# Three edits to the order and the split of ScalarE's work in a graph-attention kernel

## The chip, the cores and the metric

The kernel runs on one core of one Trainium2 chip. The metric is the device time of one execution in microseconds; lower is better. Times are medians of several runs of the same program.

## What is computed

Three attention layers over a graph of 6250 nodes (256 numbers each) and 100,000 edges (`src`, `dst`, sorted by `dst`). The first two are one GATv2 block with four heads of 64, the third is a GAT layer with eight heads of 32. After the second and the third layer the input is added and the row is normalised. Each node also has an edge from itself in the first two layers.

```python
def _gatv2_layer(x, src, dst, n, Wl, Wr, att, b):
    xl = (x @ Wl).reshape(n, H, C)
    xr = (x @ Wr).reshape(n, H, C)
    e = leaky_relu(xl[src] + xr[dst], 0.2)
    logits = einsum('ehc,hc->eh', e, att)
    ex = exp(logits - segment_max(logits, dst)[dst])
    alpha = ex / segment_sum(ex, dst)[dst]
    return segment_sum(xl[src] * alpha[:, :, None], dst).reshape(n, H * C) + b

h = elu(_gatv2_layer(x, ...))          # layer one
x = layernorm(x + _gatv2_layer(h, ...))  # layer two
x = layernorm(x + gat_layer(x, ...))     # layer three
```

## The kernel before, in words

A plan (the first 220 us) sorts the nodes by degree and cuts them into 49 blocks of 128, one node to a partition. A block has as many columns as its largest node has edges: 38 in the first block, 25, 24, 23 in the next ones, 9 in the last, 814 in all. A column is one neighbour of each of the 128 nodes.

`layer2` runs the first two layers (i = 0 and i = 1), each as one loop over the 49 blocks. The order of the instructions on every engine is the order in which the program writes them: nothing is rescheduled. In iteration b of the loop stand, in this order:

- `start(b + 3)`: layer one gathers the block's neighbour lists and inputs into `near` (x1 is the part of it with the inputs) by a GpSimd DMA; layer two loads the block's rows of two tables by SP.
- `gather(b + 1)`: one GpSimd DMA for each column of the next block, 128 rows of a table into a row tile `g` (L1207). A row tile holds up to T = 9 columns, and there are nine of them. A block of S columns (its neighbours and the node itself) is cut into chunks of equal size, at most nine columns each.
- `ready(b + 1)`: the next block's own rows. In layer one (`own1`) TensorE transposes x1 (L1254), ScalarE copies the result to `xT` (L1256), TensorE makes the products `pl` and `pr` (L1261). In layer two (`own2`) ScalarE copies both from the loaded tile. `pr` goes to PSUM; the copy of the own row into the first column of `g` is put off to `later`.
- `attend(b)`: for each chunk VectorE makes z = max(g, pr), z times the attention vector, and its sum over each head (L1396 to L1398); then the maximum over the columns (L1272). ScalarE takes the exponential of each of the four heads with the sum into `den` (L1279), copies the weights of the last `few` columns to SBUF (`by`, L1286), does what is in `later` (L1477 or L1517), and in layer one casts a column of places (L1408).
- `end(b - 1)`: VectorE scales the sum of the block before by its `den` into `h` (L1415). In layer one (`finish1`) ScalarE makes the two parts of the ELU (L1481 to L1484); in layer two (`finish2`) VectorE takes mean and variance and ScalarE makes the deviation by Ln and Exp (L1350, L1351).
- VectorE takes the reciprocal of `den` (L1447).
- `weighted_sum`: for each chunk VectorE multiplies the rows by the weights (L1309), and TensorE adds the columns up in PSUM by products with the identity (`acc`, L1316). The last `few` columns of the last chunk are multiplied by ScalarE, a head at a time (L1308). After the first chunk's product `between` calls the rest of the block before: in layer one VectorE adds the parts of the ELU (L1489), in layer two it scales the mean (L1355) and ScalarE normalises (L1358).
- `last`, of the block before: TensorE transposes h, ScalarE copies it to `xT`, TensorE makes the products with the next layer's weights, ScalarE copies these to a row (L1496, or L1531 and L1532 in layer two), and SP writes the row to the next layer's tables in HBM.

Two blocks before the end of a layer, `follow` issues the first gathers of the next layer, which read the rows of all but the last blocks (`begin`). Layer three has a loop of its own, with VectorE's sums in place of TensorE's, and isn't touched.

Of the kernel before, what the change touches and what calls it, by code (L numbers as in the profile page):

```python
# [26 lines left out]
F32 = mybir.dt.float32  # L27
# [8 lines left out]
P = 128  # L36
# [1092 lines left out]
def tile_by_degree(  # L1129
# [3 lines left out]
    nc = tc.nc  # L1133
# [3 lines left out]
    NB = -(-N // P)  # L1137
# [3 lines left out]
    W2 = H2 * (D2 + 1)  # L1141
# [16 lines left out]
    x1 = near[:, :, CM:]  # L1158
# [43 lines left out]
    def gather_rows(b, rows, cut, own, table, of, width, j0, j1):  # L1202


        for g, (s0, s1) in zip(rows, cut):
            for j in range(max(s0 - own, j0), min(s1 - own, j1)):
                nc.gpsimd.indirect_dma_start(  # L1207
                    out=g[:, j + own - s0, :width], out_offset=None, in_=table,
                    in_offset=source(of, b, j),
                )  # L1210

    def row_tiles(b, own):
        cut = chunks(cols[b] + own)
        return [rowp.tile([P, T, RW], F32, name="g") for _ in cut], cut
# [33 lines left out]
            nc.vector.reduce_sum(bad, pb, axis=AX.X)  # L1248
            nc.vector.tensor_single_scalar(done, bad, 0.0, op=OP.is_equal)

    def transposed(work, ps, xt):
        pt = ps.tile([P, 2, P], F32, name="pt", tag="tp")
        for c in range(2):
            nc.tensor.transpose(pt[:, c, :], xt[:, c * P : (c + 1) * P], ident)  # L1254
        xT = work.tile([P, 2, P], F32, name="xT")
        nc.scalar.copy(xT, pt)  # L1256
        return xT

    def product(pm, xT, w):
        for c in range(2):  # L1260
            nc.tensor.matmul(pm, xT[:, c, :], w[:, c, :], start=c == 0, stop=c == 1)  # L1261
# [6 lines left out]
    def weights(work, ps, lg, S, H, scalar=0):  # L1268


        top = work.tile([P, H], F32, name="top")
        nc.vector.tensor_reduce(  # L1272
            top, lg[:, :S, :].rearrange("p s h -> p h s"), axis=AX.X, op=OP.max, negate=True
        )
        wt = ps.tile([P, S, H], F32, name="wt")
        den = work.tile([P, H], F32, name="den")
        if H <= 4:
            for h in range(H):
                nc.scalar.activation(  # L1279
                    wt[:, :, h], lg[:, :S, h], AF.Exp, bias=top[:, h : h + 1],  # L1280
                    accum_out=den[:, h : h + 1],
                )
            by = None
            if scalar:
                by = work.tile([P, scalar, H], F32, name="by")
                nc.scalar.copy(by, wt[:, S - scalar :, :])  # L1286
            return (wt, by), lambda: den
        nc.vector.tensor_add(lg[:, :S, :], lg[:, :S, :], top[:, None, :].to_broadcast([P, S, H]))
        nc.scalar.activation(wt, lg[:, :S, :], AF.Exp)  # L1289

        def add_up():
            nc.vector.reduce_sum(den, wt.rearrange("p s h -> p h s"), axis=AX.X)
            return den

        return (wt, None), add_up
# [64 lines left out]
    def layer2(i, table, of, width, start, own, finish, follow):  # L1360

        with ExitStack() as es:
            zp = es.enter_context(tc.tile_pool(name=f"z{i}", bufs=1))
            work = es.enter_context(tc.tile_pool(name=f"work{i}", bufs=3))
            ps = es.enter_context(tc.tile_pool(name=f"ps{i}", bufs=2, space=PSUM))
            ps1 = es.enter_context(tc.tile_pool(name=f"ps1{i}", bufs=1, space=PSUM))  # L1370
            pst = es.enter_context(tc.tile_pool(name=f"pst{i}", bufs=2, space=PSUM))
            at = ps1.tile([P, W2], F32, name="at")
            nc.scalar.copy(at, att[i])
            state = {}

            def gather(b):
                first = EARLY[b] if b in begun else 0
                rows, cut = begun.pop(b) if first else row_tiles(b, 1)
                gather_rows(b, rows, cut, 1, table, of, width, first, cols[b])
                state[b] = [rows, cut]  # L1380

            later = []

            def ready(b):
                pr, put = own(work, ps, pst, b, state[b][0][0][:, 0, :W2])
                state[b].append(pr)
                later.append(put)

            def attend(b):
                rows, cut, xr = state.pop(b)  # L1390
                S = cols[b] + 1
                lg = work.tile([P, CM + 1, H2], F32, name="lg")
                for g, (s0, s1) in zip(rows, cut):
                    n = s1 - s0
                    z = zp.tile([P, T, W2], F32, name="z")[:, :n, :]
                    nc.vector.tensor_max(z, g[:, :n, :W2], xr[:, None, :].to_broadcast([P, n, W2]))  # L1396
                    nc.vector.tensor_mul(z, z, at[:, None, :].to_broadcast([P, n, W2]))  # L1397
                    nc.vector.reduce_sum(  # L1398
                        lg[:, s0:s1, :], z.rearrange("p t (h d) -> p t h d", h=H2), axis=AX.X
                    )  # L1400
                few = min(S // 3, cut[-1][1] - cut[-1][0] - 1) if b + 1 < NB else 0
                wt, new = weights(work, ps, lg, S, H2, few)
                while later:
                    later.pop()()
                if i == 0:
                    for g, (s0, s1) in zip(rows, cut):
                        s = max(s0, 1)
                        nc.scalar.copy(spots[:, b, s - 1 : s1 - 1], g[:, s - s0 : s1 - s0, W2])  # L1408
                    if 0 < b <= len(EARLY):
                        sort_sources(work, pst, b - 1)  # L1410
                return rows, cut, wt, new

            def end(b, acc, den):
                h = work.tile([P, F], F32, name="h")
                nc.vector.tensor_mul(  # L1415
                    per_head(h, H2), per_head(acc, H2),
                    den.unsqueeze(2).to_broadcast([P, H2, D2]),
                )
                if i == 0:
                    nc.vector.tensor_add(h, h, bias[0])  # L1420
                return finish(work, pst, b, h)

            for b in range(3):
                if (i, b) not in loaded:
                    start(b)
            gather(0)
            ready(0)
            later.pop()()
            if i == 0:
                none(state[0][2])  # L1430
            acc, den, rest = None, None, None
            for b in range(NB):
                if b + 3 < NB:
                    start(b + 3)
                if b + 1 < NB:
                    gather(b + 1)
                if b + 2 == NB:
                    follow()
                if b + 1 < NB:
                    ready(b + 1)  # L1440
                rows, cut, wt, new = attend(b)
                if b:
                    rest = end(b - 1, acc, den)
                if i == 0:
                    nc.vector.tensor_add(x1[:, b, :], x1[:, b, :], bias[1])
                den = new()
                nc.vector.reciprocal(den, den)  # L1447

                last = []

                def between():
                    if b:
                        last.append(rest())

                acc = weighted_sum(ps1, rows, cut, wt, H2, D2 + 1, between)
                if i == 0 and b + 1 < NB:
                    none(state[b + 1][2])
                if last:
                    last[0]()
            end(NB - 1, acc, den)()()  # L1460

    def none(t):
# [5 lines left out]
            out=near[:, b, :], out_offset=None, in_=near_d[:, :], in_offset=node(b)  # L1468
        )

    def own1(work, ps, pst, b, row):
        xT = transposed(work, pst, x1[:, b, :])
        pl = pst.tile([P, W2], F32, name="pl", tag="tp")
        product(pl, xT, wc[0][:, 0])
        pr = ps.tile([P, W2], F32, name="pr")
        product(pr, xT, wc[0][:, 1])
        return pr, lambda: nc.scalar.copy(row, pl)  # L1477

    def finish1(work, pst, b, h):
        neg = work.tile([P, F], F32, name="neg")  # L1480
# [29 lines left out]
        nc.sync.dma_start(two[:, 1, :], xr2_d[b * P : (b + 1) * P])  # L1510
        kept[b] = two

    def own2(work, ps, pst, b, row):
        two = kept.pop(b)
        pr = ps.tile([P, W2], F32, name="pr")
        nc.scalar.copy(pr, two[:, 1, :])
        return pr, lambda: nc.scalar.copy(row, two[:, 0, :])  # L1517

    def finish2(work, pst, b, h):
        nc.vector.tensor_add(h, h, x1[:, b, :])  # L1520
# [18 lines left out]
    kept, loaded = {}, set()  # L1539
# [11 lines left out]
    with ExitStack() as es:  # L1551
        work = es.enter_context(tc.tile_pool(name="work3", bufs=3))
        ps = es.enter_context(tc.tile_pool(name="ps3", bufs=3, space=PSUM))
        state = {}
# [50 lines left out]
        acc, den, puts, rest = None, None, {}, None  # L1605
        for b in range(NB):
# [4 lines left out]
            rows, cut, wt, new = attend(b)  # L1611
            if b:
                rest = end(b - 1, acc, den)
# [39 lines left out]
```

## Time and profile before

| | |
|---|---|
| median of 3 runs | 3907.3 us (3907.01 to 3914.32) |
| profiled execution | 3906.24 us, span 3904.4 us |
| layer one | 220.6 to 1476.1 us |
| layer two | 1476.1 to 2710.9 us |
| layer three | 2710.9 to 3904.4 us |
| busy over the span | VectorE 2859.7, GpSimd 2558.8, TensorE 1465.1, ScalarE 1093.2 us |
| mean granted TensorE clock | 0.669 |

The bounds of the layers are the ends of VectorE's reciprocals (L1447), of which there is one to a block: the first and the last of layer one, and the last of layer two. In a group of instructions the columns are line, engine, operation, tiles and shapes, count; then busy time and mean ns of one; then the idle time of the engine just before them, with what ended most of it. In a timeline they are start, duration, engine, line, operation, tiles, shapes and count, and in brackets the idle time before it. DVE is VectorE, ACT ScalarE, PE TensorE's matmuls, PEld its weight loads, POOL GpSimd. A releaser called "issue" or "remote" is one that the profile can't name.

### The profile page before, as it was taken

The page shows a single profiled execution, that of the slowest core. Times are in us where ns is not written, and L with a number is a line of the kernel's source. Part 1 is how long each engine was busy: PE and PEld are TensorE (multiplying, and loading weights), DVE is VectorE, ACT ScalarE, POOL GpSimd, SP SyncE. Part 2 cuts the span into 40 slices and gives each one's busy share as a digit, 9 for nine tenths or more (in the row PEclk, how much of TensorE's full clock was granted, in tenths as well). Part 3 has the DMA queues.
Part 4 walks back from the last instruction along what each step waited for, and adds up shares of the span by engine and source line. Part 5 has one row for each costly group of instructions (what it writes and reads, how often), then busy time and mean ns, then how long its engine had stood idle before and what let it go on. Part 6 is the DMA issues. An engine that isn't in the chain of part 4 may idle for free.

```text
span 3904.4 us, 23669 instructions
## 1 busy us (share of the span) xinstructions
PE 1465.1 (38%) x5147; PEld 1100.0 (28%) x5147; DVE 2859.7 (73%) x2624; ACT 1093.2 (28%) x4179; POOL 2558.8 (66%) x2642
## 2 busy tenths in 40 slices
PE   5335655646667653355545455554000000000000
PEld 4223443435455542243433334442000000000000
DVE  6267888768888867798877889895686666666655
ACT  2123433434445441243334334442000000000000
POOL 6466666666666654666666666663777777777774
PEclk8667787777888886676766777776555555555555
DMA  8443333333334333333434344342433333333332
GB/s 192 101 94 100 104 103 100 105 102 103 105 103 107 104 102 71 103 106 105 112 104 111 107 110 111 109 111 69 100 107 105 97 96 97 97 97 96 97 97 56
DMA packets 197563, 399.62 MB, mean 102 GB/s; under 512 B 63516, under 2 KB 115994, under 8 KB 197396
## 3 DMA queue, kind: packets, MB, share of 16 engines
q0 software_dynamic: 123488, 342.06, 33.7%
q1 hardware_dynamic: 66226, 54.22, 4.9%
q10 hardware_dynamic: 7698, 1.74, 0.4%
q8 instruction: 45, 0.74, 0.1%
q14 instruction: 106, 0.87, 0.1%
HBM read 357.84 MB, written 40.42 MB: 102 GB/s over the span
## 4 chain that ended last, share of the span: by engine, by line
issue 24%; POOL 21%; PE 16%; DVE 14%; another core or an unknown queue 12%; ACT 9%; DMA 2%; DVEq 0%; SPq 0%; ACTq 0%; POOLq 0%
POOL g L1207 19%; PE acc L1316 10%; ACT g L1308 4%; PE pm L1261 3%; DVE z L1397 3%; DVE z L1396 3%; DVE lg L1398 3%; ACT wt L1279 2%; DVE weighted L1327 1%; DVE g L1309 1%; DMA g<-xl_d,near_r 1%; POOL out L1597 1%; ACT xT L1256 1%; PE pl L1261 1%
## 5 line engine op out<-in xcount | busy, mean ns | idle before, releaser
L1207 POOL DMA_INDIRECT g<-xl_d,near_r x1591 | 1508.6, 948 | 843.6 <-issue 455.7
L1316 PE MATMUL acc<-g,ident 128*128 128x256 f32 x3452 | 1015.0, 455 | 910.1 <-issue 361.4
L1316 PEld LDWEIGHTS acc<-g,ident 128*128 128x128 f32 x3452 | 768.0, 229 | 1152.9 <-issue 617.4
L1207 POOL DMA_INDIRECT g<-whs_d,near_r x777 | 802.2, 1032 | 293.9 <-issue 251.9
L1308 ACT ACTIVATE g<-g,by 128x64 f32<-128x64 f32 x2064 | 550.4, 337 | 331.3 <-issue 328.0
L1396 DVE TENSOR_TENSOR z<-g,pr 128x1820 f32<-128x1820 f32 (+4 forms) x236 | 503.4, 2133 | 39.3 <-DMA g<-xl_d,near_r 25.7
L1397 DVE TENSOR_TENSOR z<-z,at 128x1820 f32<-128x1820 f32 (+4 forms) x236 | 503.7, 2134 | 8.1
L1398 DVE TENSOR_REDUCE lg<-z 128x28 f32<-128x1820 f32 (+4 forms) x236 | 503.6, 2134 | 8.1
L1336 DVE TENSOR_REDUCE acc_v<-weighted 128x256 f32<-128x4096 f32 (+16 forms) x49 | 349.2, 7127 | 11.7 <-remote 6.1
L1309 DVE TENSOR_TENSOR g<-g,wt 128x1792 f32<-128x1792 f32 (+5 forms) x236 | 353.8, 1516 | 2.9
L1567 DVE TENSOR_TENSOR lg<-g,s_r 128x56 f32<-128x56 f32 (+4 forms) x113 | 22.8, 214 | 367.4 <-DMA g<-whs_d,near_r 300.0
L1289 ACT ACTIVATE wt<-lg 128x128 f32<-128x128 f32 (+17 forms) x49 | 14.0, 285 | 901.2 <-DVE top L1272 309.9
L1256 ACT COPY xT<-pt 128x256 f32<-128x256 f32 x147 | 55.0, 374 | 704.8 <-remote 367.3
L1327 DVE TENSOR_TENSOR weighted<-g,wt 128x1792 f32<-128x1792 f32 (+4 forms) x113 | 229.5, 2048 | 0.0
L1447 DVE RECIPROCAL den<-den 128x4 f32<-128x4 f32 x98 | 17.4, 177 | 226.8 <-ACT wt L1279 158.9
L1279 ACT ACTIVATE wt<-lg,top 128x19 f32<-128x19 f32 (+14 forms) x392 | 116.1, 296 | 209.0 <-DVE top L1272 83.7
L1415 DVE TENSOR_TENSOR h<-acc,den 128x256 f32<-128x256 f32 x98 | 40.7, 416 | 166.8 <-remote 122.3
L1261 PE MATMUL pm<-wh_cat,xT 128*128 128x272 f32 x196 | 83.9, 568 | 192.7 <-issue 108.7
L1261 PE MATMUL pm<-wcat,xT 128*128 128x260 f32 x392 | 138.5, 512 | 45.8 <-ACT xT L1256 44.8
L1261 PEld LDWEIGHTS pm<-wcat,xT 128*128 128x128 f32 x392 | 96.9, 261 | 82.1 <-ACT xT L1256 61.7
L1261 PEld LDWEIGHTS pm<-wh_cat,xT 128*128 128x128 f32 x196 | 46.0, 260 | 213.5 <-issue 113.5
L1597 POOL DMA_INDIRECT out<-y,node_i x49 | 50.3, 1027 | 49.6 <-ACT y L1358 35.6
(180 smaller groups left out, 1511.1 us busy)
## 6 DMA issues: line engine op xcount, KB each, us to landing
g<-xl_d,near_r POOLq DMA_INDIRECT x1591
g<-whs_d,near_r POOLq DMA_INDIRECT x777
whs_d<-row SPq DMA_DIRECT2D x49, 132.0 KB
xl_d<-xl SPq DMA_DIRECT2D x49, 130.0 KB
xl_d<-row SPq DMA_DIRECT2D x49, 130.0 KB
xr_d<-row SPq DMA_DIRECT2D x49, 130.0 KB
two<-xl_d SPq DMA_DIRECT2D x49, 130.0 KB
two<-xr_d SPq DMA_DIRECT2D x49, 130.0 KB
```

What stands on the lines that cost most here:

```text
L1207: nc.gpsimd.indirect_dma_start(out=g[:, j + own - s0, :width], out_offset=None, in_=table, in_offset=source(of, b, j),)
L1256: nc.scalar.copy(xT, pt)
L1261: nc.tensor.matmul(pm, xT[:, c, :], w[:, c, :], start=c == 0, stop=c == 1)
L1279: nc.scalar.activation(wt[:, :, h], lg[:, :S, h], AF.Exp, bias=top[:, h : h + 1], accum_out=den[:, h : h + 1],)
L1308: nc.scalar.mul(g4[:, t, h, :], g4[:, t, h, :], by[:, t - m, h : h + 1])
L1309: nc.vector.tensor_mul(g4[:, :m], g4[:, :m], wt[:, s0 : s0 + m, :].unsqueeze(3).to_broadcast([P, m, H, F // H]),)
L1316: nc.tensor.matmul(acc, ident, g4[:, t], start=s0 + t == 0, stop=s0 + t == S - 1)
L1327: nc.vector.tensor_mul(prod[:, s0 - base : s1 - base, :].rearrange("p t (h d) -> p t h d", h=H), g[:, :n, :F].rearrange("p t (h d) -> p t ...
L1336: nc.vector.reduce_sum(part, prod[:, : s1 - base, :].rearrange("p s f -> p f s"), axis=AX.X)
L1396: nc.vector.tensor_max(z, g[:, :n, :W2], xr[:, None, :].to_broadcast([P, n, W2]))
L1397: nc.vector.tensor_mul(z, z, at[:, None, :].to_broadcast([P, n, W2]))
L1398: nc.vector.reduce_sum(lg[:, s0:s1, :], z.rearrange("p t (h d) -> p t h d", h=H2), axis=AX.X)
```

## The change

It has three edits, all in `layer2` and what it calls.

1. `own1` is cut in two. The transposes and the copy to `xT` (a tile `xo` of its own) are written two blocks ahead, between the reciprocal and `weighted_sum`. The products stay with `ready`, with `pr` ahead of `pl`.
2. `ready(b + 1)` moves from ahead of `attend(b)` into it, behind the exponentials and the copy `by`. What was `last`, called at the end of the iteration, is kept in `due` and called in the next block's `attend`, behind `ready`.
3. `few` is a sixth of the columns (S // 6) instead of a third, with the same upper limit by the last chunk's size.

```diff
-    def transposed(work, ps, xt):
+    def transposed(work, ps, xt, name="xT"):
...
-        xT = work.tile([P, 2, P], F32, name="xT")
+        xT = work.tile([P, 2, P], F32, name=name)
...
-            later = []
+            mine, due = {}, []
 
             def ready(b):
-                pr, put = own(work, ps, pst, b, state[b][0][0][:, 0, :W2])
+                pr, put = mine.pop(b)(state[b][0][0][:, 0, :W2])
                 state[b].append(pr)
-                later.append(put)
+                put()
...
-                few = min(S // 3, cut[-1][1] - cut[-1][0] - 1) if b + 1 < NB else 0
+                few = min(S // 6, cut[-1][1] - cut[-1][0] - 1) if b + 1 < NB else 0
                 wt, new = weights(work, ps, lg, S, H2, few)
-                while later:
-                    later.pop()()
+                if b + 1 < NB:
+                    ready(b + 1)
+                while due:
+                    due.pop()()
...
             gather(0)
+            for b in range(2):
+                mine[b] = own(work, ps, pst, b)
             ready(0)
-            later.pop()()
...
-                if b + 1 < NB:
-                    ready(b + 1)
                 rows, cut, wt, new = attend(b)
...
-                last = []
+                if b + 2 < NB:
+                    mine[b + 2] = own(work, ps, pst, b + 2)
 
                 def between():
                     if b:
-                        last.append(rest())
+                        due.append(rest())
 
                 acc = weighted_sum(ps1, rows, cut, wt, H2, D2 + 1, between)
                 if i == 0 and b + 1 < NB:
                     none(state[b + 1][2])
-                if last:
-                    last[0]()
+            due.pop()()
             end(NB - 1, acc, den)()()
...
-    def own1(work, ps, pst, b, row):
-        xT = transposed(work, pst, x1[:, b, :])
-        pl = pst.tile([P, W2], F32, name="pl", tag="tp")
-        product(pl, xT, wc[0][:, 0])
-        pr = ps.tile([P, W2], F32, name="pr")
-        product(pr, xT, wc[0][:, 1])
-        return pr, lambda: nc.scalar.copy(row, pl)
+    def own1(work, ps, pst, b):
+        xT = transposed(work, pst, x1[:, b, :], "xo")
+
+        def products(row):
+            pr = ps.tile([P, W2], F32, name="pr")
+            product(pr, xT, wc[0][:, 1])
+            pl = pst.tile([P, W2], F32, name="pl", tag="tp")
+            product(pl, xT, wc[0][:, 0])
+            return pr, lambda: nc.scalar.copy(row, pl)
+
+        return products
...
-    def own2(work, ps, pst, b, row):
-        two = kept.pop(b)
-        pr = ps.tile([P, W2], F32, name="pr")
-        nc.scalar.copy(pr, two[:, 1, :])
-        return pr, lambda: nc.scalar.copy(row, two[:, 0, :])
+    def own2(work, ps, pst, b):
+        def products(row):
+            two = kept.pop(b)
+            pr = ps.tile([P, W2], F32, name="pr")
+            nc.scalar.copy(pr, two[:, 1, :])
+            return pr, lambda: nc.scalar.copy(row, two[:, 0, :])
+
+        return products
```

## The prediction

> **What bounds the kernel now.** I read the busy shares by slice first, then the groups of instructions by line with what ended the idle time before them, then the timeline of single blocks, one engine at a time.
>
> ```profile
> DVE  6267888768888867798877889895686666666655
> ...
> POOL 6466666666666654666666666663777777777774
> PEclk8667787777888886676766777776555555555555
> ```
>
> Slices 3 to 28 are the two attention layers of the change (220.6 to 2710.9 us; 98 blocks). VectorE is the fullest there: 997 of 1255 us in the first, 1021 of 1235 in the second (the sums by window). GpSimd issues a gather each 1.25 us (0.95 and a gap of 0.30), some 1660 in the two layers, 2075 of 2490 us; beyond that it stalls for row buffers, so it is ahead of VectorE. So VectorE is the bound, and its idle time is what can be won.
>
> ```profile
> L1308 ACT ACTIVATE g<-g,by 128x64 f32<-128x64 f32 x2064 | 550.4, 337 | 331.3 <-issue 328.0
> ...
> L1415 DVE TENSOR_TENSOR h<-acc,den 128x256 f32<-128x256 f32 x98 | 40.7, 416 | 166.8 <-remote 122.3 <-PE acc L1316 44.4
> ...
> L1496 ACT COPY row<-pm 128x260 f32<-128x260 f32 x98 | 36.7, 374 | 130.1 <-PE pm L1261 105.6 <-issue 17.6 <-remote 6.9
> ...
> L1489 DVE SCALAR_TENSOR_TENSOR h<-neg,pos 128x256 f32<-128x256 f32 x49 | 20.6, 421 | 14.8 <-ACT pos L1484 12.4 <-ACT g L1308 2.1 <-issue 0.3
> ...
> L1531 ACT COPY row<-pm 128x264 f32<-128x264 f32 x49 | 18.6, 379 | 91.2 <-PE pm L1261 65.3 <-issue 21.4 <-remote 4.6
> ...
> L1447 DVE RECIPROCAL den<-den 128x4 f32<-128x4 f32 x98 | 17.4, 177 | 226.8 <-ACT wt L1279 158.9 <-issue 67.9
> ```
>
> Two waits hold VectorE's idle time: L1447 (the exponentials) with 226.8 us, L1415 (the sum that TensorE adds up) with 166.8. L1489, which waits for the ELU's parts, has 14.8. One block of the first layer, ScalarE alone, shows where the first comes from:
>
> ```profile
> 871.61 0.37 ACT L1256 COPY xT<-pt 128x256 f32<-128x256 f32 x1 [2.85 <-PE pt L1254]
> 874.17 0.38 ACT L1496 COPY row<-pm 128x260 f32<-128x260 f32 x1 [2.19 <-issue]
> 875.20 0.37 ACT L1496 COPY row<-pm 128x256 f32<-128x256 f32 x1 [0.65 <-PE pm L1261]
> 875.47 0.38 ACT L1256 COPY xT<-pt 128x256 f32<-128x256 f32 x1
> 875.73 0.31 ACT L1279 ACTIVATE wt<-lg,top 128x18 f32<-128x18 f32 x1
> ```
>
> The maxima are ready at 872.86, but the exponential starts at 875.73, behind the round trip of the last-but-one step: transposes, products, copies. VectorE has 1.1 us of other work and then waits 3.56 us for `den`.
>
> **The skill.** "TensorE: Matmul & The Clock Gate", section "Architectural detail: the array is 16× 32×32", calls ScalarE and VectorE strict FIFO. The lines above agree: nothing behind the copies starts. Its section "What's actually happening" says that the matmul clock is halved after an idle window of about 3.4 us. Here the granted clock takes the values 0.5 and 1.0 alone, in stretches that are multiples of 3.41 us, mean 0.669. "Perfetto Trace Analysis", section "Tensor Engine Instruction", calls matmul times in a profile a model; this trace agrees: in the block at 2018.9 us the last matmul is recorded at 31.4, and VectorE's h starts at 48.5 (both after 2000). So TensorE is timed below by who waits for it. "ScalarE: Activation LUTs", section "What ACT_TABLE_LOAD costs", gives 280 ns and 0.833 ns an element with one pointer operand: 333 ns for 64 elements, and L1308 shows 337.
>
> **The change, step by step.** Blocks have S columns, one more than gathered, S from 39 to 10.
>
> *A. Exponentials first.* Four of them take 1.8 us from the maxima (875.73 to 877.54). Late blocks, where ScalarE is free already, leave 0.66 us at L1447 in layer one (the reciprocal at 1419.22) and 0.33 in layer two (the one at 2608.14; more VectorE work in between). L1447 has 145.5 and 81.3 us in the layers; 49 x 0.66 and 49 x 0.33 stay, so 113 + 65 = 178 us go. One wait of 12.4 us, at the end of layer one, is a slow product that is waited for elsewhere then: **-166 us**.
>
> *B. What is late next.* The round trip isn't removed: `due` now stands behind the exponentials and ahead of `end` in ScalarE's order, so that it starts only when the maxima are there, whenever TensorE is done. Its first copy waits for the transposes, the later ones for products that themselves wait for the first. Queued behind them on ScalarE: the casts, Relu, Exp, Relu of L1481 to L1484 (layer one), Ln and Exp of L1350 and L1351 (layer two), and then ScalarE's products. VectorE needs the parts at L1489 and the deviation at L1355, right after the first product with the weights; behind these stand the products of the other chunks, the next block's z and, through them, TensorE's sum. From E, the end of the exponentials, in layer one: copy of own row at E+0.08, xT at E+0.35, first copy of pm 2.56 later (871.61 to 874.17), second 1.03 later, casts at E+4.2, Relu E+4.6, parts done E+5.75. VectorE: reciprocal 0.2, product 2.27 (the mean first chunk of 7.2 columns), ready at E+2.5. Stall 3.3 us, where there is none now. The two copies wait 2.65 us a block in the mean (twice 130.1/98), 2.84 in this block and 3.55 in the block at 846 us: 3.1 to 4.0. Before the trip TensorE will have idled, so I take 3.5. Layer two: two copies, xT at E+0.7, L1531 2.64 later (2048.54 to 2051.18), Ln at E+3.7, Exp done E+4.2, VectorE ready at E+2.3: 1.9; with the mean wait of L1531 (91.2/49 = 1.86 against 2.27 there) 1.55, with a short first chunk and the slow trip 2.3. I take 1.9. Blocks 2 to 48: 47 x (3.5 + 1.9) = **+254 us**, ends 219 and 296. It can't go below nothing: nothing hides it but VectorE's 2.3 us, counted already.
>
> *C. A sixth instead of a third.* With the chunks' limits ScalarE's columns fall from 258 to 122 a layer, so L1308 from 2064 to 976 instructions. VectorE takes 272 columns more, at (2553 - 946)/6 = 268 ns each (the product's forms of 9 and 3 columns): **+73 us**, all on the bound engine.
>
> *D. What fewer ScalarE products return.* They are off the path, but TensorE waits for them before its last columns. L1415 waits 61.4 us in layer one, where ScalarE's products stretch (328 us of idle time inside L1308), and 99.6 in layer two, mostly single waits of 10 to 27 us in which TensorE itself is late. Bounds: all 161 go; or up to 20 more, since a late sum now also delays the trip and then the parts. I take half of layer one, and 2 us off each of some dozen waits of layer two, as the stall gives TensorE that time: **-55 us**.
>
> *At nothing.* Transposing own rows a block ahead (two transposes and a copy, all moved) needs x1 of block b+2, whose gather GpSimd issues before those of block b, so it has landed; it puts 0.6 us of TensorE ahead of the sum and 0.4 us of ScalarE ahead of its products, both beside VectorE's z. The products pr and pl (four records each, 1.0 and 1.1 us) now come as soon as the sum before is done, beside z too; without that cover they cost 2.2 us a block. Of what `due` moves, the two table writes of SP go out later: they are independent of the loads of `two` between them, but at the layers' ends GpSimd's early gathers, which read these rows, wait some 6 us more. GpSimd waits 23.9 us later there for the last row, which covers it; else 6 us at each of two ends. No new function is used, so no table load comes in.
>
> **Sum** against the profiled execution (3906.2 us, span 3904.4): -166 + 254 + 73 - 55 = +106, so 4012; the median stands 1 us above it: **4013 us**, 3960 to 4065 for this case.
>
> **Rivals.**
> *TensorE freed.* ScalarE's columns are what makes TensorE late; with half of them all of L1415's 161 us go, and trips run at the low price. -166 + 219 + 73 - 161 = -35: 3872, faster. For it: in blocks 4 to 21 the sum ends just after ScalarE's last product. Against: the 25 us wait at the end of layer two comes with 12 products. It decides from D over 126 us, at that B. Chance 0.19.
> *TensorE stays late.* D is 0: 4068. For it: the long waits stand beside a clock of 0.64 to 0.68, and the change takes no matmul away. Chance 0.24.
> *Not first after all.* ScalarE's products overrun the maxima in layer one, so only layer two gains: -65 + 254 + 73 = +262, 4169. Against: they end 2 us before the maxima even now. Chance 0.04.
> The forecast has 0.53. A tenth lies below 3890 and a tenth above 4090. Faster 0.17 (the first rival, less 0.02), within 0.2% (about what a measurement can tell) 0.03, slower 0.80.
>
> **What would show it.** A: L1447's line falls to some 50 to 60 us. B: the step of L1489 stands idle 3 to 4 us a block and that of L1355 near 2, released by ScalarE. C: VectorE's busy time up by some 73 us. D: L1415's line near 110. I am wrong if the ELU's parts don't become the next wait, or if L1415's line empties.

## The result and the profile after

| | before | after |
|---|---|---|
| median of 4 runs | 3910.8 us (3907.0 to 3917.7) | 4052.8 us (4039.3 to 4065.7) |
| profiled execution | 3906.2 us, span 3904.4 | 4065.7 us, span 4063.7 |
| layer one, blocks 4 to 46 | 1049.5 us | 1155.6 us |
| layer two, blocks 51 to 96 | 1067.8 us | 1118.8 us |
| layer three | 1193.5 us | 1192.9 us |
| VectorE busy | 2859.7 us | 2937.5 us |
| ScalarE busy | 1093.2 us | 790.5 us |

The changed kernel takes 1.037 times the time of the kernel before (95% interval 1.034 to 1.040), 142 us more. The stretches of layers are between VectorE's reciprocals, as before.

The experiments below ran on three chips, and the kernel before doesn't take the same time on all of them: 3404 and 3407 us on two, 3922 us on the third, much as in the first measurement. So each ratio is against runs of the kernel before on the same chip, and I call the two kinds the 3404 chips and the 3910 chips. Each of the three was met on one occasion only, so whether the chip or the occasion makes the difference isn't shown. The only profile of the kernel before is that of the first measurement; the profiles set against it below may be from another 3910 chip.

I start with the busy shares by slice.

```profile
DVE  6276788768877775698886898888296656656654
...
POOL 6466666666555535566666665654577777777774
```

VectorE is still the fullest engine of the two layers, and no fuller than before in spite of 78 us more work: the time has come out as idle time. The groups of instructions say where.

```profile
L1309 DVE TENSOR_TENSOR g<-g,wt 128x1792 f32<-128x1792 f32 (+6 forms) x236 | 426.8, 1823 | 1.8
...
L1308 ACT ACTIVATE g<-g,by 128x64 f32<-128x64 f32 x976 | 250.1, 337 | 50.5 <-issue 49.0 <-DMA g<-xl_d,near_r 1.0
...
L1418 DVE TENSOR_TENSOR h<-acc,den 128x256 f32<-128x256 f32 x98 | 40.7, 415 | 158.7 <-remote 122.8 <-PE acc L1316 35.9
...
L1502 ACT COPY row<-pm 128x260 f32<-128x260 f32 x98 | 36.6, 374 | 164.6 <-PE pm L1261 86.0 <-issue 78.5
...
L1495 DVE SCALAR_TENSOR_TENSOR h<-neg,pos 128x256 f32<-128x256 f32 x49 | 20.9, 426 | 201.7 <-ACT pos L1490 161.1 <-issue 30.5 <-ACT g L1308 5.9
...
L1540 ACT COPY row<-pm 128x264 f32<-128x264 f32 x49 | 18.5, 378 | 110.3 <-PE pm L1261 58.0 <-issue 52.3
...
L1449 DVE RECIPROCAL den<-den 128x4 f32<-128x4 f32 x98 | 17.2, 176 | 48.5 <-ACT wt L1279 27.1 <-issue 21.4
...
L1355 DVE SCALAR_TENSOR_TENSOR sd<-mv,sd 128x1 f32<-128x1 f32 x98 | 15.3, 156 | 92.6 <-ACT sd L1351 29.5 <-ACT row L1540 24.1 <-issue 18.5
```

Before, the line of the mean's scaling was this:

```profile
L1355 DVE SCALAR_TENSOR_TENSOR sd<-mv,sd 128x1 f32<-128x1 f32 x98 | 15.2, 155 | 1.8 <-ACT sd L1351 1.8
```

The reciprocal's line (L1449, L1447 before) has fallen from 226.8 to 48.5 us. The step of the ELU add (L1495, L1489 before) has risen from 14.8 to 201.7 us, and that of the mean's scaling (L1355) from 1.8 to 92.6. The sum's line (L1418, L1415 before) has hardly moved: 166.8 before, 158.7 now, though ScalarE makes 976 products in place of 2064. VectorE's own products with the weights (L1309) take 426.8 us, 353.8 before. ScalarE's own waits for the round trip are no shorter than before (L1502 164.6 us, L1496 before 130.1; L1540 110.3, L1531 before 91.2), but now VectorE stands behind them. One block of layer one shows the new wait, ScalarE first and then VectorE.

```profile
829.24 0.29 ACT L1279 ACTIVATE wt<-lg,top 128x18 f32<-128x18 f32 x1 [12.05 <-DVE top L1272]
...
831.04 0.17 ACT L1286 COPY by<-wt 128x12 f32<-128x12 f32 x1
832.47 0.38 ACT L1481 COPY g<-pl 128x260 f32<-128x260 f32 x1 [1.26 <-PE pl L1261]
832.89 0.37 ACT L1256 COPY xT<-pt 128x256 f32<-128x256 f32 x1
835.19 0.38 ACT L1502 COPY row<-pm 128x260 f32<-128x260 f32 x1 [1.93 <-PE pm L1261]
836.07 0.37 ACT L1502 COPY row<-pm 128x256 f32<-128x256 f32 x1 [0.50 <-PE pm L1261]
...
837.55 0.40 ACT L1490 ACTIVATE pos<-h 128x256 f32<-128x256 f32 x1
```

```profile
831.32 2.52 DVE L1309 TENSOR_TENSOR g<-g,wt 128x2304 f32<-128x2304 f32 x1
...
837.98 0.42 DVE L1495 SCALAR_TENSOR_TENSOR h<-neg,pos 128x256 f32<-128x256 f32 x1 [4.12 <-ACT pos L1490]
```

The exponentials stand first and aren't held up (the 12.05 us ahead of them are the wait for the maxima). Then come the own row, after a wait of 1.26 us for TensorE, and the three copies of the round trip, with waits of 1.93 and 0.50 us, and only behind these the ELU's parts, the last at 837.55. VectorE had finished the first product with the weights 4.12 us before it could go on.

The books of the two profiled executions: 78 us more of work, 187 at L1495, 91 at L1355, less 178 at L1449 and 8 at L1418, is 170. The span grew by 159; the other lines give back some 10.

### The profile page after: what moved, and what is told of

Its sections match the earlier page's. It is cut to its first block, busy times and chain, and to the rows that moved or that the text cites. A ratio compares the mean times of both kernels' runs of the same rounds, so it can differ in the third digit from the quotient of the medians.

```text
span 4063.7 us, 22403 instructions
## 1 busy us (share of the span) xinstructions
PE 1364.5 (34%) x5147; PEld 1096.1 (27%) x5147; DVE 2937.5 (72%) x2624; ACT 790.5 (19%) x3091; POOL 2555.1 (63%) x2642
## 4 chain that ended last, share of the span: by engine, by line
DVE 36%; issue 22%; POOL 19%; PE 8%; ACT 7%; another core or an unknown queue 4%; DMA 3%; DVEq 0%; ACTq 0%; SPq 0%; POOLq 0%
POOL g L1207 18%; DVE z L1397 10%; DVE z L1398 10%; DVE lg L1399 8%; PE pm L1261 4%; ACT wt L1279 3%; DVE g L1309 3%; PE acc L1316 3%; DMA g<-xl_d,near_r 2%; DVE weighted L1327 1%; POOL out L1606 1%; PE pm L835 1%; DVE top L1272 1%; DMA g<-whs_d,near_r 1%
## 5 line engine op out<-in xcount | busy, mean ns | idle before, releaser
L1316 PE MATMUL acc<-g,ident 128*128 128x256 f32 x3452 | 878.8, 414 | 267.3 <-DVE g L1309 133.3
L1316 PEld LDWEIGHTS acc<-g,ident 128*128 128x128 f32 x3452 | 725.9, 213 | 416.6 <-DVE g L1309 148.6
L1397 DVE TENSOR_TENSOR z<-g,pr 128x1820 f32<-128x1820 f32 (+4 forms) x236 | 503.4, 2133 | 44.0 <-DMA g<-xl_d,near_r 33.4
L1309 DVE TENSOR_TENSOR g<-g,wt 128x1792 f32<-128x1792 f32 (+6 forms) x236 | 426.8, 1823 | 1.8
L1261 PE MATMUL pm<-wcat,xT 128*128 128x260 f32 x392 | 178.6, 634 | 549.6 <-ACT xT L1256 225.6
L1261 PE MATMUL pm<-wh_cat,xT 128*128 128x272 f32 x196 | 105.9, 695 | 620.2 <-ACT xT L1256 348.4
L1261 PEld LDWEIGHTS pm<-wcat,xT 128*128 128x128 f32 x392 | 119.6, 320 | 589.1 <-ACT xT L1256 231.5
L1308 ACT ACTIVATE g<-g,by 128x64 f32<-128x64 f32 x976 | 250.1, 337 | 50.5 <-issue 49.0
L1261 PEld LDWEIGHTS pm<-wh_cat,xT 128*128 128x128 f32 x196 | 57.1, 321 | 643.2 <-ACT xT L1256 355.0
L1495 DVE SCALAR_TENSOR_TENSOR h<-neg,pos 128x256 f32<-128x256 f32 x49 | 20.9, 426 | 201.7 <-ACT pos L1490 161.1
L1418 DVE TENSOR_TENSOR h<-acc,den 128x256 f32<-128x256 f32 x98 | 40.7, 415 | 158.7 <-remote 122.8
L1355 DVE SCALAR_TENSOR_TENSOR sd<-mv,sd 128x1 f32<-128x1 f32 x98 | 15.3, 156 | 92.6 <-ACT sd L1351 29.5
```

The lines of the kernel that those rows point to most:

```text
L1308: nc.scalar.mul(g4[:, t, h, :], g4[:, t, h, :], by[:, t - m, h : h + 1])
L1309: nc.vector.tensor_mul(g4[:, :m], g4[:, :m], wt[:, s0 : s0 + m, :].unsqueeze(3).to_broadcast([P, m, H, F // H]),)
L1316: nc.tensor.matmul(acc, ident, g4[:, t], start=s0 + t == 0, stop=s0 + t == S - 1)
```

## The experiments

**Theory and rivals.** The theory: the cost is VectorE's extra columns (edit 3) and two stalls that come from where `due` stands (edit 2), and undoing both should leave the gain at the exponentials. Rival one: ScalarE's smaller share is what costs, in one way or another. Rival two: what waits is TensorE, and wherever a wait is taken away, another one takes its place.

**First four, on a 3404 chip.** Their expectations were written with the first measurement's times in mind; where they name a time, it is to be read here as a difference from the kernel before, 3404.0 us.

*The changed kernel with a third of the columns* (edits 1 and 2 without 3):

```diff
-                few = min(S // 6, cut[-1][1] - cut[-1][0] - 1) if b + 1 < NB else 0
+                few = min(S // 3, cut[-1][1] - cut[-1][0] - 1) if b + 1 < NB else 0
```

> The changed kernel with the share of ScalarE back at a third (S // 3). Theory: VectorE's busy time falls by the 73 to 78 us of the 272 columns and the time by about as much, to some 3975; L1495 and L1355 keep their stalls of 200 and 90 us; L1418 stays within 40 us of its 159. Rival (half the products of ScalarE freed TensorE, so taking them back makes it late): L1418 grows by over 60 us and the time stays above 4020.

Measured: 3696.1 us, ratio 1.085 (1.084 to 1.087), 292 us slower than the kernel before.

```profile
L1495 DVE SCALAR_TENSOR_TENSOR h<-neg,pos 128x256 f32<-128x256 f32 x49 | 20.9, 426 | 196.1 <-ACT pos L1490 196.1
...
L1355 DVE SCALAR_TENSOR_TENSOR sd<-mv,sd 128x1 f32<-128x1 f32 x98 | 15.5, 158 | 95.4 <-ACT sd L1351 95.4
```

The two idle times are 291.5 us together. So without edit 3 the two stalls are nearly the whole loss, and nothing is won at the exponentials: their line has 52.1 us here, and the run of edit 1 alone, below, has no more.

*The changed kernel with `due` behind the end of the block before* (a sixth of the columns):

```diff
                     ready(b + 1)
-                while due:
-                    due.pop()()
...
                     rest = end(b - 1, acc, den)
+                while due:
+                    due.pop()()
```

> The changed kernel with one thing moved: what is kept in due is written behind end(b - 1) instead of ahead of it, so that ScalarE makes the ELU's parts (layer one) and the deviation (layer two) before the round trip of products and copies. Theory (the new stall is the place of due in ScalarE's order): the idle time before L1495 falls from 202 to below 25 us and that before L1355 from 93 to below 10, L1449 keeps some 50, and the time falls by 230 to 280 us, to about 3790, below both kernels. Rival (the trip then holds TensorE's sum back, and the stall comes out at L1418): L1418 grows from 159 to over 300 us and the time stays above 3900.

Measured: 3486.4 us, ratio 1.024 (1.022 to 1.026), 210 us less than the run above in spite of the dearer split.

```profile
L1495 DVE SCALAR_TENSOR_TENSOR h<-neg,pos 128x256 f32<-128x256 f32 x49 | 20.6, 421 | 4.0 <-ACT pos L1490 3.8
...
L1355 DVE SCALAR_TENSOR_TENSOR sd<-mv,sd 128x1 f32<-128x1 f32 x98 | 15.0, 153 | 1.8 <-ACT sd L1351 1.8
```

Both stalls are gone, with the same copies and the same products, only behind the ELU's parts and the deviation in ScalarE's order. The copies of the trip wait as long as in the run above (L1502 167.8 us in both), so it is the place of `due` that costs, not the round trip itself. Against the kernel before with edit 3 alone, the next run, this order is still 10 us slower.

*The kernel before with a sixth of the columns* (edit 3 alone):

```diff
-                few = min(S // 3, cut[-1][1] - cut[-1][0] - 1) if b + 1 < NB else 0
+                few = min(S // 6, cut[-1][1] - cut[-1][0] - 1) if b + 1 < NB else 0
```

> The kernel before with the third edit alone (S // 6). Theory: VectorE's busy time up by 73 to 78 us; since the sum ends some us earlier, less of the trip is still in front of the exponentials, so L1447 falls somewhat, from 227 to 150 to 200 us; L1415 stays near 160; time 3930 to 3980. Rival (ScalarE's columns are what makes TensorE late): L1415 falls below 60 us and the time comes to 3870 or below.

Measured: 3476.8 us, ratio 1.021 (1.020 to 1.023), 73 us more. VectorE's products with the weights take 426.3 us where the kernel with a third takes 353.9, and no line of idle time answers.

*The kernel before with own rows transposed ahead* (edit 1 alone):

```diff
+            for b in range(2):
+                mine[b] = own(work, ps, pst, b)
...
-                pr, put = own(work, ps, pst, b, state[b][0][0][:, 0, :W2])
+                pr, put = mine.pop(b)(state[b][0][0][:, 0, :W2])
...
+                if b + 2 < NB:
+                    mine[b + 2] = own(work, ps, pst, b + 2)
```

> The kernel before with the first edit alone: own rows transposed and copied a block ahead, everything else in its old place. Theory: the exponentials of layer one lose one copy and one transpose in front of them, 0.3 to 0.7 us a block, so L1447 falls by 15 to 35 us and the time by as much, to about 3885. Rival (the transposes ahead of the sum hold TensorE back): L1415 grows and the time stays at 3905 or above.

Measured: 3405.1 us, ratio 1.000 (0.999 to 1.001). Edit 1 costs nothing, as the prediction had it, and brings nothing: the 15 to 35 us that the expectation names didn't come where the exponentials hardly wait. Its profile also stands in for the kernel before on such a chip.

```profile
L1415 DVE TENSOR_TENSOR h<-acc,den 128x256 f32<-128x256 f32 x98 | 40.6, 414 | 10.0 <-PE acc L1316 10.0
...
L1449 DVE RECIPROCAL den<-den 128x4 f32<-128x4 f32 x98 | 17.4, 178 | 52.2 <-ACT wt L1279 52.2
```

ScalarE's products have no gap here. The reciprocal waits 52.2 us, and with the exponentials first it waited as long (52.1 us, in the changed kernel with a third of the columns). So this is the floor on such a chip, and there is nothing that edit 2 could win.

**Four on a 3910 chip** (kernel before 3921.7 us).

*The changed kernel again.*

> The changed kernel itself beside the kernel before, on the chip of this call. Theory: edits one and two cost the stall at L1495 and L1355 (some 290 us) less what L1447 has above its floor of 50 us; edit three costs 73 us. Where the kernel before takes some 3404 us, L1447 is at its floor and the change costs 290 + 73: about 3767, ratio 1.107. Where it takes some 3907, L1447 gives back 178: about 4055, ratio 1.04. Rival (the cost is a share of the time, whatever the waits): a ratio of 1.035 to 1.04 in both.

Measured: 4060.9 us, ratio 1.035 (1.031 to 1.039), with 49.0, 207.5, 92.3 and 158.2 us at L1449, L1495, L1355 and L1418. This is the first measurement again.

*`due` behind the end, a third of the columns* (the second edit shown above, with S // 3): both losses of the theory undone, the gain kept.

> The changed kernel with due behind end(b - 1) and the share back at a third: exponentials first and own rows ahead, without the two parts that cost. Theory: no stall at L1495 and L1355, L1449 at its floor: where the kernel before takes 3404, within 0.5% of it (nothing is left to win); where it takes 3907, the 178 us of L1447 less what L1418 keeps: 3700 to 3780. Rival (holding the trip back a block costs by itself): slower than the kernel before by over 0.5% on either.

Measured: 3923.7 us, ratio 1.0005 (0.998 to 1.003). My expectation of some 3700 to 3780 us fell, and with it the half of the theory which said that the gain would be left.

```profile
L1308 ACT ACTIVATE g<-g,by 128x64 f32<-128x64 f32 x2064 | 522.9, 340 | 143.5 <-issue 138.7 <-DMA g<-xl_d,near_r 4.2
...
L1416 DVE TENSOR_TENSOR h<-acc,den 128x256 f32<-128x256 f32 x98 | 41.2, 420 | 401.6 <-remote 291.0 <-PE acc L1316 76.6 <-PE pt L1254 14.7
...
L1495 DVE SCALAR_TENSOR_TENSOR h<-neg,pos 128x256 f32<-128x256 f32 x49 | 21.1, 430 | 19.7 <-ACT pos L1490 11.4 <-issue 6.0 <-ACT neg L1487 2.0
...
L1449 DVE RECIPROCAL den<-den 128x4 f32<-128x4 f32 x98 | 16.6, 169 | 20.9 <-ACT wt L1279 14.0 <-issue 6.9
```

The reciprocal waits 20.9 us and the ELU add 19.7: both won. But h, the next instruction that needs TensorE, waits 401.6 us, 235 more than in the profile of the kernel before. The order alone doesn't do it: with the same order (and a sixth of the columns) h waited 12.9 us on the 3404 chip. So I read it thus: on this kind of chip TensorE's sum comes late, and the wait at the exponentials had covered for it. This is what rival two says; why TensorE is late isn't shown.

*The same with half the columns*: `few = min(S // 2, ...)`, 321 columns a layer in place of 258.

> The same with ScalarE weighting half of the columns (S // 2, within the last chunk's limit: 321 columns a layer instead of 258). Theory: VectorE is the bound and ScalarE has room, so 126 columns in both layers at 268 ns go from the path: 34 us faster than with a third. Rival (ScalarE's products then hold TensorE's sum back): L1418 grows by over 34 us and nothing is won.

Measured: 3912.1 us, ratio 0.997 (0.996 to 0.999). VectorE's busy time is 34 us less than in the run above, but h waits 415.2 us, 14 more, and the ELU add 40.3, 21 more, so that the time falls by 12 us only. A quarter more products on ScalarE makes the sum only that little later: ScalarE's columns can be no more than a small part of what makes TensorE late.

*The kernel before with pauses on GpSimd.* In the trace of the kernel before, TensorE's completions come in a burst some 2.5 to 4 us after GpSimd has begun to wait for row buffers (waits from 700.6, 727.2 and 763.5 us, bursts at 703.0, 730.4 and 767.7), and slowly while it issues gathers back to back. So I let it do eight small instructions of its own in the middle of each block:

```diff
+                if own and j == cols[b] // 2:
+                    for _ in range(8):
+                        nc.gpsimd.iota(rest_t, pattern=[[1, 200]], base=0, channel_multiplier=0,
+                                       allow_small_or_imprecise_dtypes=True)
```

> The kernel before with eight short instructions of GpSimd in the middle of each block's gathers, so that it issues no gather for some 3 us there. Where the kernel before takes 3907, theory (TensorE's and ScalarE's completions are held up while GpSimd issues gathers one after the other, and come in bursts when it stalls): L1447 and L1415 together fall by over 100 us and the kernel is faster by 50 or more. Rival (TensorE is slow by itself): both stay, and the time grows by nothing to 60 us. Where the kernel before takes 3404, there is no such wait to remove, and GpSimd is close to VectorE: 50 to 200 us slower.

Measured: 4002.2 us, ratio 1.021 (1.018 to 1.025), 80 us slower, which is more than the rival allowed. (Line numbers of `layer2` are five higher in it.)

```profile
L1420 DVE TENSOR_TENSOR h<-acc,den 128x256 f32<-128x256 f32 x98 | 40.9, 418 | 187.3 <-remote 160.0 <-PE acc L1321 27.3
...
L1452 DVE RECIPROCAL den<-den 128x4 f32<-128x4 f32 x98 | 17.4, 178 | 260.0 <-ACT wt L1284 190.1 <-issue 69.9
```

In the profile of the kernel before, h waits 166.8 us and the reciprocal 226.8: the pauses don't bring TensorE's sums forward, and my guess about GpSimd isn't borne out. ScalarE's products have 105.6 us of gaps in place of 331.3, but this can't be put down to the pauses: as many products without pauses have 143.5 on this chip, in the run with `due` behind the end. The cause of the late completions stays open.

**The last four, on another 3404 chip** (kernel before 3407.5 us).

*The changed kernel a third time.*

> The changed kernel a third time. My theory is that its cost is edit 3 (73 us, everywhere) and the two new stalls in front of the ELU add and the mean's scaling (278 to 292 us, everywhere), and that the 178 us won at the exponentials are there only on an occasion on which ScalarE's and TensorE's steps are stretched by waits that the profile can't name. So: ratio 1.035 to 1.04 if the kernel before takes some 3910 us here, 1.10 to 1.11 (365 us more) if it takes some 3404. The rival (the cost is one constant, some 3.7 per cent, and the first four experiments met something else) says 1.037 in either case.

Measured: 3769.8 us, ratio 1.106 (1.105 to 1.108), 362 us slower. This is what the theory says for such a chip; a constant 3.7 per cent is out.

```profile
L1418 DVE TENSOR_TENSOR h<-acc,den 128x256 f32<-128x256 f32 x98 | 40.6, 414 | 5.5 <-PE acc L1316 5.5
...
L1495 DVE SCALAR_TENSOR_TENSOR h<-neg,pos 128x256 f32<-128x256 f32 x49 | 20.8, 425 | 194.7 <-ACT pos L1490 194.7
...
L1449 DVE RECIPROCAL den<-den 128x4 f32<-128x4 f32 x98 | 17.4, 178 | 52.4 <-ACT wt L1279 52.4
...
L1355 DVE SCALAR_TENSOR_TENSOR sd<-mv,sd 128x1 f32<-128x1 f32 x98 | 15.4, 157 | 95.4 <-ACT sd L1351 95.4
```

Against the kernel with own rows ahead on a chip of this kind: 73.0 us for the columns, 7 of other work, 191.1 at L1495 and 93.6 at L1355, less 4.5 at L1418, is 360; the spans differ by 363. The timeline of one round trip, ScalarE and then TensorE, shows the price of the stall without the disturbance of the 3910 chip.

```profile
729.57 0.38 ACT L1481 COPY g<-pl 128x260 f32<-128x260 f32 x1
729.84 0.39 ACT L1256 COPY xT<-pt 128x256 f32<-128x256 f32 x1
732.42 0.38 ACT L1502 COPY row<-pm 128x260 f32<-128x260 f32 x1 [2.19 <-PE pm L1261]
734.15 0.37 ACT L1502 COPY row<-pm 128x256 f32<-128x256 f32 x1 [1.36 <-PE pm L1261]
```

```profile
730.28 3.83 PE L1261 MATMUL pm<-wcat,xT 128*128 128x260 f32 x8 [13.36 <-ACT xT L1256]
```

And the window around it: start and end, length, busy time and count on each engine, then TensorE's granted clock, DMA share and GB/s.

```profile
729.60:734.20 4.60, 3.92 (x10) 3.04 (x11) 1.85 (x3) 1.05 (x5) 3.38 (x5) 0.50 0.49 134
```

Here is a trip of the kernel with own rows ahead, on the other 3404 chip, where it stands at the end of the iteration:

```profile
729.57 0.37 ACT L1256 COPY xT<-pt 128x256 f32<-128x256 f32 x1 [5.32 <-PE pt L1254]
731.18 0.38 ACT L1504 COPY row<-pm 128x260 f32<-128x260 f32 x1 [1.23 <-PE pm L1261]
732.05 0.37 ACT L1504 COPY row<-pm 128x256 f32<-128x256 f32 x1 [0.50 <-PE pm L1261]
```

In the changed kernel the own row and xT go at once from the end of the exponentials (about 729.5), the first copy of pm comes 2.58 us after xT, the second 1.73 us after that. With the trip at the end of the iteration these are 1.61 and 0.87 us, at a clock of 1.00 through the trip, right behind the matmuls of the sum. So the new place doesn't only put the trip in front of VectorE, it also makes it 1.83 us longer. In the kernel before, in the first measurement, the second came 0.88 us after the first in the median block. The clock is 0.50 through the changed kernel's trip: by the records TensorE had no matmul for 13.36 us ahead of it. That agrees with the Trainium skill, "TensorE: Matmul & The Clock Gate", section "What's actually happening", by which the clock is halved after an idle window.

*`due` behind the end with half the columns, here too.*

> Edits 1 and 2 with the delayed steps behind the end of the block before, ScalarE weighting half the columns (321 a layer instead of 258): the same kernel as measured at 0.9973. If VectorE's 63 columns a layer fewer (126 by 268 ns, 34 us) are the whole of it: 0.990 where the kernel before takes 3404 us, 0.997 where it takes 3910, since there TensorE's lateness takes most of it. If the order is what won: the same here as there, and better than the kernel before with half the columns, which runs beside it.

Measured: 3397.5 us, ratio 0.997 (0.996 to 0.998), 10 us faster and not 34. h waits 12.5 us only, but the first step of a chunk (L1397) 56.9, where it has 41.9 in the kernel with own rows ahead. The ratio is that of the 3910 chip, with another wait in the place of TensorE's.

*Edit 1 and half of edit 2*: the own row behind the exponentials, the round trip at the end of the iteration as before, a third of the columns.

```diff
-                while due:
-                    due.pop()()
...
                     none(state[b + 1][2])
-            due.pop()()
+                if due:
+                    due.pop()()
```

> Half of edit 2 with a third of the columns: the own row's products and copy behind the exponentials, but the round trip of h called at the end of the iteration as before, ahead of the next exponentials. If it is the round trip's copies that hold the exponentials back (my reading of the timeline), the reciprocal's line stays near the 227 us of before where the kernel before takes 3910 us, and the ELU add has no stall (some 15 us): 3900 to 3920. If the own row's copies are what holds them back, the line falls to some 60 us and the time by up to 160. Where the kernel before takes 3404 us the line is at its floor of 52 us anyway and both give 3404.

Measured: 3407.7 us, ratio 1.000 (0.999 to 1.001), no stall at the ELU add (3.6 us), 51.9 at the reciprocal, which is the floor of this chip. So the own row's new place alone costs nothing; whether it is the own row or the round trip that held the exponentials back on a 3910 chip isn't decided, since this run didn't fall on one.

*The kernel before with half the columns*: `few = min(S // 2, ...)`, nothing else.

> The kernel before with ScalarE weighting half of the columns instead of a third, nothing else: 126 columns fewer on VectorE by 268 ns, 34 us less where nothing answers. If ScalarE's products then overrun the maxima or make TensorE late, the waits of the reciprocal and of h grow by as much or more: same or slower. I expect 0.991 where the kernel before takes 3404 us; where it takes 3910, the same within 0.3 per cent, because ScalarE's stretched products come ahead of the round trip and of the exponentials there.

Measured: 3392.5 us, ratio 0.9955 (0.994 to 0.997), 15 us faster where I had expected some 30.

```profile
L1396 DVE TENSOR_TENSOR z<-g,pr 128x1820 f32<-128x1820 f32 (+4 forms) x236 | 503.5, 2133 | 56.1 <-DMA g<-xl_d,near_r 47.9 <-DMA near_r<-near_d,node_i 1.2 <-ACT g L1517 0.8
```

VectorE's products shrink by 34 us (320.2 against 353.9 with a third), but the first step of a chunk waits 56.1 us where it waited 41.9 with a third, mostly for the gathered rows: VectorE begins to catch up with GpSimd. Of the new order nothing is needed for this gain; the order with half the columns is 5 us slower beside it. It is the best kernel of the study on a 3404 chip, and wasn't tried on a 3910 chip.

## Why the prediction was right, and where its sizes were off

The direction was right, and so was the mechanism of A, B and C; D failed. The time is 40 us above the forecast of 4013. The span grew by 159 us, not 106: against the sum's terms A brought 12 us more, B cost 24 more and D brought 47 less, so only A's 12 us cancelled other errors. Step by step:

*A, exponentials first.* 178 us were to go from L1447; 178.3 went. The 12.4 us that I took back for a slow product which is waited for elsewhere can't be seen in a line of its own.

*B, what is late next.* The two places were the ones named, L1489 and L1355, but the stalls are 278 us, against 254. Layer two is right: 90.8 us, 1.9 a block. Layer one has 186.9 us, 4.0 a block, against 3.5. The mis-sized term is the second copy of pm, taken at 1.03 us after the first from a block of the kernel before. Moved behind the exponentials the trip mostly follows a stretch in which TensorE has nothing to do, and runs at the halved clock: 1.73 us in the median block, in this trace and in the one on a 3404 chip, both times with a granted clock of 0.50 (the block shown from this trace, with 0.88, is one of the others). The forecast's own sentence "Before the trip TensorE will have idled" was the reason to take this end for every block, and I took the middle; the 3.3 us of the working with 0.70 more for this copy are the 4.0.

*C, the columns.* 73 us forecast, 73.0 measured in L1309's busy time, 72.9 by the run with edit 3 alone.

*D, what fewer products return.* This step failed: 55 us were to come off L1415, 8 came. I had put half of layer one's wait down to ScalarE's products, since they were stretched and TensorE needs them. (The 328 us of stretching that the working gives for layer one are those of both layers; layer one has 293.5.) In layer one ScalarE now makes 488 products in place of 1032, with 33.0 us of gaps, and yet h waits 73.4 us there, where it waited 61.4. With `due` behind the end 2064 products give 401.6 us at h and 2568 give 415.2. So the number of products has little to do with it; what makes the sum late stays open. The old order with fewer products wasn't run on a 3910 chip. The rival "TensorE stays late" had D at nothing and 4068 us, and comes closest to what happened.

*At nothing.* Own rows ahead: ratio 1.000 (on a 3404 chip). The later table writes: layer three takes as long as before (1192.9 against 1193.5 us).

*A reading of the trace.* The 17 us between the last recorded matmul (2031.4) and h (2048.5) were taken as agreeing with matmul times being a model. On a 3404 chip h waits 10.0 us in all 98 blocks together, so a gap of this size goes with the 3910 chips and says nothing of how matmul times are made.

What the working didn't have is that its terms aren't independent on such a chip. A sum of A, B, C and D reads as if A's 178 us were kept once B is mended. The run with `due` behind the end and a third of the columns says otherwise: mending B takes out 278 us of stall there, C another 74 and the reciprocal 28, and the time falls by 137 only, because h then waits 243 us more. On the 3404 chips the same move of `due` was kept in full: 283 us, from 3769.8 to 3486.4, where the two stalls had 290. So I read the wait at the exponentials and the wait for the sum, on a 3910 chip, as two places at which VectorE waits for the same late chain. That is a reading; no run tests it by itself. The rival "TensorE freed" fell with D.

That the loss is 142 us on one chip and 362 us on another fits this: B and C are paid on both, A is there to be won only where the steps of ScalarE and TensorE are stretched. The forecast holds for the kind of chip whose profile it was read from; that there is another kind, this profile couldn't tell.

## What to carry to other kernels

In an engine that works strictly in order, putting one thing first decides what is last: before moving a wait out of the way of one consumer, list who stands behind its new place and price each with the slow case of the trip, since the move itself may bring TensorE into the halved clock. A wait that is taken away is worth what it was only if the producer behind the next wait is early; where several waits go back to one late engine, they can't be added. And where a line's idle time has no releaser that the profile can name, see whether it is there on another chip before it is counted as something to win.

## What the runs showed of the hardware that was not expected

The same program takes 3404 to 3407 us on two chips, and 3922 us on a third, much like the 3911 of the first measurement. A large part of the difference lies in waits without a named cause: ScalarE's products have 331.3 us of gaps on one kind and none on the other, h waits 166.8 us against 10.0, the reciprocal 226.8 against 52.2, and a gather of layer three takes 1032 ns against 949 (802.2 us for 777 of them, against 737.7). VectorE's own work is the same to 2 us (2859.7 and 2858.3). (The figures of the second kind are those of the kernel with own rows ahead.)

The bursts of TensorE's completions, described with the pauses, go with the kind of chip. If a burst is six or more completions at most 0.06 us apart, the profile of the kernel before has 72 of them, that of the changed kernel 20, the four on the 3910 chip of the experiments 25 to 74, and the eight on 3404 chips none. That is no cause shown: with the pauses there are still 59.
